# Two stages of a hybrid layer in other forms: neighbourhood attention in larger query tiles, and the spectral products with other PSUM buffers

## The chip, the cores and the metric

The kernel runs on one core of a Trainium2 chip. The metric is the device time of one execution in microseconds (us); for the kernel before it is the median of three runs. Engines are named as in the profile: PE multiplies matrices (PEld is its weight load), DVE and ACT work on vectors, POOL is the general engine, SP issues most DMAs.

## The reference, cut to what matters

The input is four images of 56 x 56 tokens with 128 channels. Each image goes through three residual steps:

```python
# group norm over the image (32 groups), then 7x7 neighbourhood attention, 4 heads of 32:
q, k, v = split(norm(x) @ qkv_w.T + qkv_b)
attn = softmax(einsum("bnhwd,bnhwkd->bnhwk", q, k_win) * SCALE + bias)
x += einsum("bnhwk,bnhwkd->bnhwd", attn, v_win) @ proj_w.T + proj_b
# layer norm, then linear attention with exp features:
q, k, v = exp(h @ Wq + bq), exp(h @ Wk + bk), h @ Wv + bv
x += einsum("bnu,buv->bnv", q, einsum("bnu,bnv->buv", k, v))
# layer norm, then a mixture of experts (hard choice of one of 4) of a spectral filter:
#   16 long causal filters along the 3136 tokens, each with two 128x128 matrices (plus, minus),
#   and an autoregressive part of 3 taps with 128x128 matrices
out = spectral(h, sigma, phi, M_plus, M_minus) + ar(M_u, h)
```

The long convolution is done as a transform over 42 x 56 points: rows first (42 frequencies), then for each of the 42 frequencies a stage with tokens, filters and matrices, then back.

## The kernel before, in words

All data are float32. There are four stages. The *preparation* chooses the expert, forms the filter matrices `mats` in SBUF and the transformed filters `vd` in DRAM. Then each *image* is worked on in turn (`project`, `row_transforms` of the image before, `attend`, `mix`). Then comes the *spectral stage*, 42 iterations. The *last stage* transforms back, adds the stored `td` and writes the output.

*Image.* `load_image` brings an image as `acc` (two buffers, the next image while this one is mixed). `project` turns tokens to channels (`to_channels`, L527), takes group statistics, normalizes, and makes keys `kp` (L658), queries `qT` (L670) and values (L684, L688); the values are stored in DRAM as `vpad`, with a border of zeros. `attend` walks over 35 tiles of 8 rows by 12 or 8 columns. For tile n, `weigh` loads the values of the window from `vpad` in two halves of seven rows (`v_sb`), multiplies the scores of four heads (`sp`, L723, four row groups of the array side by side), adds the bias and takes the maximum in one DVE instruction per head (L736), exponentiates with a sum on ACT (L747) and scales on POOL (L758). `turn_over` transposes the scores of one key half (L770) and copies them (L774, DVE or ACT), `collect` multiplies with the values (L785) and copies the output (L792). PE's order is written out: in step n PE turns over the first half of tile n-2, weighs tile n, turns over the second half of n-2 and collects n-3. Score buffers `st` are four. `mix` adds the projection to `acc` (L543, L552), normalizes (`normed`: statistics on DVE, ten small POOL instructions per block of 512 tokens, normalizing on ACT at L594, all pipelined by block), mixes (L824 to L846), and does the same again for the autoregressive part (L560), storing `ud` and `td` block by block. `row_transforms(b)` reads `ud` back as `uin`, multiplies with `into` (L505), copies `xs` and stores it in `xd`; for image b it stands after the projection of image b+1. Outside the two parts with PE's order written out, a planner orders each engine's instructions: the earliest in the program that it thinks ready.

*Spectral stage.* Iteration `it` has eight steps `eh`. In each, `matrices` makes a sixteenth of the filter matrices' 64 rows by 16 matmuls (L934, four row groups) in two tiles `pg`, each two PSUM banks, one buffer per tile; DVE copies one tile and ACT the other into `gt` (L943). Then come seven `product`s of the iteration before (L953): sixteen rows of `py` in quadrant m2 % 4, two accumulating matmuls each. After sixteen products `gather` copies the four quadrants of the `py` bank (two buffers) to `ys`, by ACT and DVE in turn (L966). `token_points` runs in steps 1 and 3 (L916, copies L924 and L925), `columns` for iteration `it - 3` in step 5 (two matmuls, L989, each with a copy on ACT, L996, through one bank). `regroup` takes `ys` through DRAM (`yd`) to `yg`.

Of the kernel before, what the change touches and what calls it, by code (L numbers as in the profile page):

```python
# [21 lines left out]
QR, QC = 8, 12  # L22
WIDTHS = (12, 12, 12, 12, 8)
# [3 lines left out]
KH = KR // 2  # L27
KMAX = KH * KC
# [92 lines left out]
def hybrid_kernel(  # L121
# [33 lines left out]
    vpad = tc.dram_tile([B, HP, WP, C], F32, name="vpad")  # L155
# [10 lines left out]
    main = ctx.enter_context(ExitStack())  # L166

# [206 lines left out]
    with main as ph:  # L374
        wts = ph.enter_context(tc.tile_pool(name="wts", bufs=1, reuse_waits="tile"))
        res = ph.enter_context(tc.tile_pool(name="res", bufs=2, reuse_waits="tile"))
        img = ph.enter_context(tc.tile_pool(name="img", bufs=1, reuse_waits="tile"))
        work = ph.enter_context(tc.tile_pool(name="work", bufs=2, reuse_waits="tile"))
        small = ph.enter_context(tc.tile_pool(name="small", bufs=4, reuse_waits="tile"))
        ps_s = ph.enter_context(tc.tile_pool(name="ps_s", bufs=3, space=bass.MemoryType.PSUM, reuse_waits="tile"))  # L380
        ps_t = ph.enter_context(tc.tile_pool(name="ps_t", bufs=1, space=bass.MemoryType.PSUM, reuse_waits="tile"))
        ps_m = ph.enter_context(tc.tile_pool(name="ps_m", bufs=1, space=bass.MemoryType.PSUM, reuse_waits="tile"))

        turn = [0]

        def bank():

            turn[0] = (turn[0] + 1) % 4
            if turn[0] == 3:
                return ps_m.tile([P, 512], F32, tag="m", name="bm")  # L390
            return ps_s.tile([P, 2, 512], F32, tag="s", name="bs")[:, 0, :]

        def load_image(b):

            acc = res.tile([P, NB, 2 * C], F32, name="acc")
            nc.sync.dma_start(
                acc[:, : NB - 1, :],
                xt[b, : 256 * (NB - 1)].rearrange("(j p f) c -> p j (f c)", p=P, f=2),
            )
            nc.sync.dma_start(  # L400
                acc[:TAIL, NB - 1, :],
                xt[b, 256 * (NB - 1) :].rearrange("(p f) c -> p (f c)", f=2),
            )
            return acc

        accs = {0: load_image(0)}


        wqkv = wts.tile([P, 3 * C], F32, name="wqkv")
        nc.scalar.dma_start(wqkv, qkv_wT)  # L410
        bqkv = wts.tile([P, 2], F32, name="bqkv")
        with nc.allow_non_contiguous_dma(reason="256 biases, a partition each"):
            nc.scalar.dma_start(bqkv, qkv_b[: 2 * C].rearrange("(s p) -> p s", p=P))
        nc.vector.tensor_scalar(bqkv[:, 0:1], bqkv[:, 0:1], HD ** -0.5, None, ALU.mult)
        bval = wts.tile([P, C], F32, name="bval")
        nc.scalar.dma_start(bval, qkv_b[2 * C :].partition_broadcast(P))
# [5 lines left out]

        relb = {}
        for qc in sorted(set(WIDTHS)):
            kc = qc + KS - 1
            relb[qc] = wts.tile([QR * qc, NH, KR * kc], F32, name=f"relb{qc}")
            for h in range(NH):
                for qy in range(QR):
                    at = (h * BIAS_H + QR - 1 - qy) * BIAS_W + QC - qc
                    nc.scalar.dma_start(  # L430
                        relb[qc][qy * qc : (qy + 1) * qc, h, :],
                        bass.AP(
                            rel_bias.tensor,
                            rel_bias.offset + at,
                            [[1, qc], [BIAS_W, KR], [1, kc]],
                        ),
                    )
# [7 lines left out]
        bkv = wts.tile([P, 2 * C], F32, name="bkv")  # L445
        nc.scalar.dma_start(bkv[:, :C], bk.partition_broadcast(P))
        nc.scalar.dma_start(bkv[:, C:], bv.partition_broadcast(P))
        into = wts.tile([P, 2 * N1], F32, name="into")
        nc.scalar.dma_start(into, table["into"])


# [676 lines left out]
```

## Time and profile before

| | |
|---|---|
| median of three runs | 2739.52 us (2738.39 to 2740.39) |
| the profiled execution's own time | 2739.52 us |
| its span, first to last instruction | 2737.7 us |
| granted TensorE clock, mean | 0.771 |
| busy: PE, PE weight loads, DVE, ACT, POOL | 2069.0, 1419.4, 1331.0, 1072.3, 694.2 us |
| preparation; images; spectral stage; last stage | about 148; 1345; 1094; 151 us |

The stages are cut by eye from the chain of work that ended last. A view of groups gives, for each line of the program, engine and tile, the busy time, the mean of one instruction and the idle time just before it with what ended it; the view of waits sums that idle time by pair; the timeline lists instructions by start; the view of windows gives busy time by engine in a stretch. Matmul durations overlap, so a matmul's cost on the path is read from the distance between starts.

### The profile page before, as it was taken

The numbers are of one execution on the slowest core, as the hardware profiler recorded it, in microseconds if no ns is written. First come the engines' busy times: TensorE is split into PE (matmuls) and PEld (weight loads), VectorE is DVE, ScalarE is ACT, GpSimd is POOL, SyncE is SP. The second block draws the span as 40 slices with busy tenths as digits, with TensorE's granted clock in tenths as the row PEclk, the third lists the DMA queues.
The fourth block names the chain that finished last, engine by engine and source line by source line (L and its number), as shares of the span: only waits on it lengthen the run. The fifth ranks groups of instructions, "written<-read, shape, count | busy, mean of one in ns | idle before, by whom it ended". The sixth has DMA issues, their size and how long they took to land.

```text
span 2737.7 us, 67019 instructions
## 1 busy us (share of the span) xinstructions
PE 2069.0 (76%) x28284; PEld 1419.4 (52%) x28284; DVE 1331.0 (49%) x3228; ACT 1072.3 (39%) x2521; POOL 694.2 (25%) x1227
## 2 busy tenths in 40 slices
PE   3066687666776677776686888888888888888598
PEld 3034456244563445534463767666766666676322
DVE  5244445444454443444432556555555655555232
ACT  0034433344424444244441455555555555555200
POOL 1146734376424664257630000000000000000000
PEclk7565579555885557855585899999999999999755
DMA  6620003300043000420015233333333333333497
GB/s 163 144 88 26 27 1 106 100 26 23 9 113 88 27 19 14 111 66 26 16 44 139 42 81 81 81 81 79 89 78 86 81 86 76 76 80 65 105 229 199
DMA packets 219519, 210.11 MB, mean 77 GB/s; under 512 B 43154, under 2 KB 187250, under 8 KB 218642
## 3 DMA queue, kind: packets, MB, share of 16 engines
q1 hardware_dynamic: 197850, 189.31, 27.9%
q10 hardware_dynamic: 21368, 16.51, 2.3%
q8 instruction: 222, 3.64, 0.5%
q14 instruction: 79, 0.65, 0.1%
HBM read 116.32 MB, written 89.45 MB: 75 GB/s over the span
## 4 chain that ended last, share of the span: by engine, by line
PE 42%; ACT 19%; DVE 18%; DMA 9%; issue 6%; POOL 5%; SPq 1%; ACTq 1%; DVEq 0%; POOLq 0%
ACT st L747 8%; PE pg L934 7%; DVE ys L966 7%; PE py L953 6%; PE sp L723 6%; ACT ys L966 5%; DVE gt L943 5%; PE pt L770 4%; PE bs L543 4%; ACT gt L943 3%; PE po L1059 2%; DMA xd<-xs 2%; DVE st L736 2%; PE pz L989 2%; PE pu L916 2%
## 5 line engine op out<-in xcount | busy, mean ns | idle before, releaser
L758 POOL TENSOR_SCALAR st<-st,rec 96x252 f32<-96x252 f32 (+1 forms) x560 | 484.9, 880 | 370.9 <-DVE rec L756 216.5
L943 DVE COPY gt<-pg 128x896 f32<-128x896 f32 x336 | 366.7, 1091 | 288.4 <-PE pg L934 279.1
L934 PE MATMUL pg<-v,mats 32*128 32x112 f32 x10752 | 398.9, 286 | 103.2 <-DVE gt L943 86.1
L934 PEld LDWEIGHTS pg<-v,mats 32*128 32x128 f32 x10752 | 338.5, 190 | 192.4 <-DVE gt L943 167.1
L747 ACT ACTIVATE st<-st,nmx 96x252 f32<-96x252 f32 (+1 forms) x560 | 270.4, 484 | 351.2 <-DVE nmx L736 351.2
L943 ACT COPY gt<-pg 128x896 f32<-128x896 f32 x336 | 304.4, 906 | 244.7 <-PE pg L934 233.5
L770 PE MATMUL pt<-ident,st 96*126 96x96 f32 (+1 forms) x1120 | 233.8, 360 | 214.6 <-ACT p L774 162.6
L953 PE MATMUL py<-gt,us 128*16 128x128 f32 x9408 | 389.7, 283 | 2.5 <-DVE gt L943 1.6
L770 PEld LDWEIGHTS pt<-ident,st 96*126 96x126 f32 (+1 forms) x1120 | 159.4, 207 | 347.0 <-POOL st L758 252.1
L953 PEld LDWEIGHTS py<-gt,us 128*16 128x16 f32 x9408 | 295.0, 112 | 67.4 <-issue 31.1
L966 DVE COPY ys<-py 16x512 f32<-16x512 f32 (+1 forms) x336 | 209.5, 624 | 160.2 <-ACT ys L966 157.8
L736 DVE CUSTOM_DVE_ANT_0 st<-sp,relb 96x252 f32<-96x252 f32 (+1 forms) x560 | 195.3, 400 | 87.8 <-PE sp L723 87.1
L966 ACT COPY ys<-py 16x512 f32<-16x512 f32 (+1 forms) x336 | 174.6, 520 | 149.2 <-DVE ys L966 141.1
L723 PE MATMUL sp<-kp,qT 32*96 32x252 f32 (+1 forms) x1120 | 162.2, 647 | 3.3 <-DVE xs L185 1.8
L774 DVE COPY p<-pt 126x384 f32<-126x384 f32 (+1 forms) x140 | 74.2, 530 | 160.3 <-PE pt L770 160.3
L594 ACT ACTIVATE hn<-acc,v 128x128 f32<-128x128 f32 (+1 forms) x208 | 88.1, 484 | 153.2 <-POOL v L586 138.9
L1059 PE MATMUL po<-z,onto 84*56 84x512 f32 x224 | 126.0, 1066 | 21.8 <-DMA z<-zd 21.8
L989 PE MATMUL pz<-yg,back 112*112 112x512 f32 x168 | 96.5, 657 | 46.3 <-ACT zs L996 36.2
L785 PE MATMUL po<-p,v_sb 126*32 126x96 f32 (+1 forms) x2240 | 112.6, 349 | 0.8 <-DVE aT L792 0.8
L505 PE MATMUL px<-uin,into 28*84 28x512 f32 x224 | 77.0, 960 | 36.2 <-DVE xs L185 19.7
L747 ACT ACTIVATION_READ_ACCUMULATOR st<-st,nmx 96x1 f32 (+1 forms) x560 | 104.4, 186 | 0.0
L1068 DVE SCALAR_TENSOR_TENSOR tl<-po,hmask,tl 56x512 f32<-56x512 f32 x56 | 42.0, 750 | 124.3 <-PE po L1059 123.7
(162 smaller groups left out, 2221.3 us busy)
## 6 DMA issues: line engine op xcount, KB each, us to landing
xd<-xs SPq DMA_DIRECT2D x112, 168.0 KB
xm<-xd SPq DMA_DIRECT2D x84, 224.0 KB
yd<-ys SPq DMA_DIRECT2D x168, 112.0 KB
yg<-yd SPq DMA_DIRECT2D x84, 224.0 KB
zd<-zs SPq DMA_DIRECT2D x84, 224.0 KB
z<-zd SPq DMA_DIRECT2D x14, 1344.0 KB
v_sb<-vpad SPq DMA_DIRECT2D x224, 63.0 KB
vpad<-vt SPq DMA_DIRECT2D x56, 112.0 KB
```

Of the source, the lines that this page charges most:

```text
L723: nc.tensor.matmul(sp[h // 2][:nq, h % 2, : 2 * kn], qT[hs, ty, QR * x0 : QR * x0 + nq], kp[hs, y0 : y0 + KR, x0 : x0 + kc], start=True, s ...
L736: nc.vector.tensor_tensor_reduce(st[:nq, h, : 2 * kn], sp[h // 2][:nq, h % 2, : 2 * kn], relb[qc][:, h], -1.0, 3.0e38, ALU.add, ALU.min, n ...
L747: nc.scalar.activation(st[:nq, h, : 2 * kn], st[:nq, h, : 2 * kn], AF.Exp, bias=nmx[:nq, h : h + 1], scale=-1.0, accum_out=ssum[:nq, h : h ...
L758: nc.gpsimd.tensor_scalar(st[:nq, h, : 2 * kn], st[:nq, h, : 2 * kn], rec[:nq, h : h + 1], None, ALU.mult)
L770: nc.tensor.transpose(pt[:kn, h, :nq], st[:nq, h, c * kn : (c + 1) * kn], ident[:nq, :nq])
L785: nc.tensor.matmul(po[hs], v_sb[:kn, c, hs], pc[c][:kn, h, :nq], start=(c == 0), stop=(c == 1),)
L934: nc.tensor.matmul(pg[g // 2][:, g % 2, 2 * N2 * i : 2 * N2 * (i + 1)], mats[rows, 4 * eh + i, :], v[rows], start=True, stop=True,)
L943: copy(gt[:, :, e0 : e0 + 8, :].rearrange("p m (g i) c -> p g m i c", g=2), pg[q][:, :, : 8 * N2].rearrange("p g (i m c) -> p g m i c", i= ...
L953: nc.tensor.matmul(py[32 * j : 32 * j + 2 * NSB, slot, :], us[:, 1 - c : 3 - c, :, m2], gt[:, m2, :, c], start=(c == 0), stop=(c == 1),)
L966: (nc.vector.tensor_copy if j % 2 else nc.scalar.copy)(ys[rows, 4 * q : 4 * q + n], py[rows, :n])
L989: nc.tensor.matmul(pz, tables_of(m1)[2], yg[:, s * B : (s + 1) * B].rearrange("p k e -> p (k e)"), start=True, stop=True,)
L1059: nc.tensor.matmul(po[64 * q : 64 * q + H].rearrange("p b c -> p (b c)"), onto[:, s], zin[q][:, i, s], start=(s == 0), stop=(s == NS - 1),)
```

## The change

Both the image stage and the spectral stage take other forms.

*Images.* All four images are loaded at the very start into one `acc`. Attention has 28 tiles of 8 x 14 queries; the keys of a tile are 14 x 20 and are turned over in three chunks of 5, 5 and 4 rows. Values stay in SBUF as `vp` in channels; for each tile POOL copies the window, PE transposes it in three parts, and DVE copies the result. Scores are taken two heads at a time; one DVE instruction scales and adds the bias for both, one takes the maximum, ACT exponentiates, DVE scales. PE's order in attention is left to the planner. A layer norm takes all statistics of the image first (DVE), then one power (POOL), then normalizes all blocks (DVE). `row_transforms(b)` stands at the end of image b, and `td` is stored in two DMAs just before it.

*Spectral.* `pg` has three rotating buffers of two banks, of which a step uses two; each is copied by DVE (one bank) and ACT (the other). `py` has one buffer; products come eight at a time in steps 0 to 6, with 32 columns of `us` (16 wanted, 16 of other rows or zeros) so that all 128 rows of the bank are written, and one full-width copy, alternating between ACT and DVE, takes the bank. `columns` does one half in step 5 and one in step 7, with alternating copies, and shares its bank with `token_points`.

```diff
-QR, QC = 8, 12
-WIDTHS = (12, 12, 12, 12, 8)
+QR, QC = 8, 14
...
+    acc = keep1.tile([P, NB, B, 2 * C], F32, name="acc")
+    for b in range(B):
+        nc.sync.dma_start(acc[:, : NB - 1, b, :], xt[b, : 256 * (NB - 1)]...)
...
+        ps_s = ...bufs=2  ps_t = ...bufs=2  ps_m = ...bufs=2      (ps_s tiles are two banks)
...
+        def layer_norm(b, to):
+            for j in range(NB):
+                r = rows_of(j)
+                for f in range(2):
+                    g = 2 * j + f
+                    nc.vector.bn_stats(stats[:r, g, :], acc[:r, j, b, f * C : (f + 1) * C])
+                    nc.vector.bn_aggr(mv[:r, g, :], stats[:r, g, :])
+            nc.gpsimd.tensor_scalar(rstd, mv[:, :, 1], LN_EPS, None, ALU.add)
+            nc.gpsimd.tensor_tensor(rstd, rstd, mhalf, ALU.pow)
+            for js in BLOCKS:
+                hn = work.tile([P, 2, 2, C], F32, name="hn")
...
+                        nc.vector.tensor_scalar(hn[...], acc[...], mv[:r, g, 0:1],
+                            rstd[:r, g : g + 1], ALU.subtract, ALU.mult)
+                to(js, lambda j, f: hn[:r, j - js[0], f, :], hn)
...
+            def weigh(ty, tx):
+                vt = work.tile([P, KR, KC], F32, name="vt")
+                nc.gpsimd.tensor_copy(vt, vp[:, y0 : y0 + KR, x0 : x0 + KC])
+                pv = ps_m.tile([KMAX, len(RCH), C], F32, tag="m", name="pv")
+                for c, nr in enumerate(RCH):
+                    nc.tensor.transpose(pv[: nr * KC, c, :], vt[...], ident)
+                nc.vector.tensor_copy(v_sb[:, 0:2, :], pv[:, 0:2, :])
+                nc.vector.tensor_copy(v_sb[:nk2, 2, :], pv[:nk2, 2, :])
+                for hp in range(NH // 2):
+                    sp = ps_s.tile([NQ, 2, 512], F32, tag="s", name="sp")
+                    for hh in range(2):
+                        nc.tensor.matmul(sp[:, hh, :NK], qT[hs, ty, tx]..., kp[hs, ...], ...)
+                    st = work.tile([NQ, 2, NK], F32, name="st")          # two buffers
+                    nc.vector.scalar_tensor_tensor(st, sp[:, :, :NK], HD ** -0.5, relb[...], ALU.mult, ALU.add)
+                    nc.vector.tensor_reduce(nmx, st, AX.X, ALU.max, negate=True)
+                    for hh in range(2):
+                        nc.scalar.activation(st[:, hh, :], st[:, hh, :], AF.Exp, bias=..., accum_out=...)
+                    nc.vector.reciprocal(rec, ssum)
+                    for hh in range(2):
+                        nc.vector.tensor_scalar(st[:, hh, :], st[:, hh, :], rec[:, hh : hh + 1], None, ALU.mult)
+                    pt0 = ps_t.tile([KMAX, 2, 2, NQ], F32, tag="t", name="pt0")
+                    pt1 = ps_t.tile([nk2, 2, NQ], F32, tag="t", name="pt1")
...                                                       (six transposes into pt0 and pt1)
+                    nc.scalar.copy(p0, pt0)
+                    nc.vector.tensor_copy(p1, pt1)
...
+            for ty in range(H // QR):
+                for tx in range(W // QC):
+                    now = weigh(ty, tx)
+                    if before is not None:
+                        collect(*before)
+                    before = now
...
+            layer_norm(b, autoregress)
+            nc.sync.dma_start(td[b, ...], acc[:, : NB - 1, b, :])
+            nc.sync.dma_start(td[b, ...], acc[:TAIL, NB - 1, b, :])
+            row_transforms(b)
...
-        ps_g = ...bufs=1     ps_y = ...bufs=2
+        ps_g = ...bufs=3     ps_y = ...bufs=1
...
-            for q, copy in enumerate((nc.vector.tensor_copy, nc.scalar.copy)):
-                e0 = 16 * eh + 8 * q
-                copy(gt[:, :, e0 : e0 + 8, :]..., pg[q][:, :, : 8 * N2]...)
+            for q in range(2):
+                for g, copy in enumerate((nc.vector.tensor_copy, nc.scalar.copy)):
+                    e0 = 16 * eh + 8 * q + 4 * g
+                    copy(gt[:, :, e0 : e0 + 4, :], pg[q][:, g, : 8 * N2]...)
...
-                    py[32 * j : 32 * j + 2 * NSB, slot, :],
-                    us[:, 1 - c : 3 - c, :, m2],
+                    py[32 * j : 32 * (j + 1), slot, :],
+                    us.rearrange("p c k m -> p (c k) m")[:, NSB * (1 - c) : NSB * (5 - c), m2],
...
+                    if eh in (5, 7) and 0 <= az < N1:
+                        columns(az, ygs[az], zs, eh // 6)
+                    if 0 <= ap < N1 and eh < 7:
+                        if eh % 2 == 0:
+                            py = ps_y.tile([P, 4, C], F32, name="py")
+                        for m2 in range(8 * eh, 8 * eh + 8):
+                            product(py, gts[ap], us2[ap % 2], m2)
+                        if eh % 2 or eh == 6:
+                            q, n = eh // 2, 2 if eh == 6 else 4
+                            evacuate(ys[:, 4 * q : 4 * q + n], py[:, :n])
```

## The prediction

> **What bounds the kernel now.** I read the busy times by window first, with the windows cut where the chain of waits changes its lines. The columns are: window, its length, busy us of PE, PE's weight loads, DVE, ACT and POOL, then the granted clock, DMA share and GB/s.
>
> ```profile
> 182.00:348.00 166.00, 112.13 (x1031) 66.77 (x1034) 80.38 (x401) 79.19 (x303) 118.22 (x136) 0.51 0.09 25
> 348.00:452.00 104.00, 85.05 (x524) 66.80 (x521) 42.78 (x125) 37.78 (x91) 41.02 (x146) 0.83 0.12 37
> 452.00:511.00 59.00, 41.96 (x166) 19.98 (x164) 26.80 (x46) 13.29 (x23) 8.80 (x13) 0.73 0.54 147
> 1530.00:2550.00 1020.00, 898.01 (x20319) 704.55 (x20314) 603.48 (x731) 522.07 (x810) 0.00 (x0) 1.00 0.35 78
> ```
>
> These are attention of image 0, its two norms with the mixing between, projection of image 1 with the row transforms of image 0, and the spectral stage. Images 1 to 3 repeat the first three (attention 170, 166, 167; projection 59, 59, 57). So 148 us of preparation, about 1345 for the images, 1094 for the spectral stage (1493 to 2587), 151 for the end. In attention POOL is the busiest (118 of 166: `L758`, 0.9 us each, four a tile) and no engine is full: 35 tiles take 4.8 us each at half clock. In the spectral stage PE is busy 88% at full clock, so I looked at the waits there (who waited for whom: us in total, times, longest):
>
> ```profile
> DVE ys L966 <- ACT ys L966: 157.8, 289, 4.2
> ACT ys L966 <- DVE ys L966: 141.1, 166, 1.2
> PEld pg L934 <- DVE gt L943: 167.1, 252, 3.5
> PEld pz L989 <- ACT zs L996: 72.7, 42, 2.3
> ACT xs L183 <- DMA xd<-xs: 86.8, 23, 6.6
> ```
>
> The timeline of one iteration shows how they hang together (start, us, what):
>
> ```profile
> 1910.75 0.57 ACT L966 COPY ys<-py 16x512 f32<-16x512 f32 x1
> 1911.03 0.98 PEld L934 LDWEIGHTS pg<-v,mats 32*128 32x128 f32 x32 [0.37 <-DVE gt L943]
> 1911.03 1.16 PE L934 MATMUL pg<-v,mats 32*128 32x112 f32 x32
> 1911.35 0.68 DVE L966 COPY ys<-py 16x512 f32<-16x512 f32 x1 [0.37 <-ACT ys L966]
> 1912.07 0.58 ACT L966 COPY ys<-py 16x512 f32<-16x512 f32 x1 [0.75 <-DVE ys L966]
> ...
> 1912.67 0.70 DVE L966 COPY ys<-py 16x512 f32<-16x512 f32 x1 [0.64 <-ACT ys L966]
> 1913.40 1.09 DVE L943 COPY gt<-pg 128x896 f32<-128x896 f32 x1
> ```
>
> The four quarter copies of one product bank go one after another, ACT, DVE, ACT, DVE, 2.6 us from 1910.75 to 1913.37. DVE's copy of the filter matrices, whose matmuls ended at 1912.1, starts only at 1913.40, and with one pair of banks per half the next matrices wait for it. The first token-point matmul comes at 1900.67 and again at 1925.85: 25.2 us an iteration.
>
> [...] the quarter copies are in different quadrants and still take turns. [...] 128x448 from PSUM takes 0.62 us (`L924`), 128x1024 in SBUF 0.75 (`L296`)[...].
>
> **The change, part by part.**
>
> *Spectral stage.* One iteration's PE work after the change: eight sets of filter matrices at 1.09 us (1902.84 to 1903.93, no stall), eight; seven groups of products instead of eight. A group of seven products takes 1.09 (1901.75 to 1902.84) and its longest quadrant has two products; a group of eight has two in each quadrant, so it also costs 1.09. Then two token-point blocks at 1.07 and two column matmuls at about 0.95. Sum 8.7 + 7.6 + 2.1 + 1.9 = 20.4. The stationary operand of a product grows from 16 to 32 columns. [...] I take 0.4, since in attention 32-column loads of `po` show matmuls exactly one stream apart (0.160 us). With 0.8 us of small gaps: 21.6 us against 25.2, 3.6 x 42 = **-151**. The copies do not stand in the way: DVE has sixteen 128x448 at 0.62, two 128x512 at 0.69, two `us` at 0.62 and one `zs` at 0.6, 13.2 us; ACT sixteen at 0.55 and the rest, about 11. A pair of banks is free 0.75 us after its matrices (0.1 + 0.62), and 1.09 of products or 0.95 of columns cover that; if both engines lag, the third pair covers one more. The single `py` bank must be emptied within the 1.09 of the next matrices (0.7 needed). Ends: -175 if no gap is left, -110 if loads and waits keep 1 us more.
>
> *Attention.* 28 tiles of 112 queries by 280 keys in place of 35 of at most 96 by 252. At half clock, from the trace's spacing: a transpose costs 0.160 for 96 columns, so 0.187 for 112 and 0.213 for 128; a score pass 0.528 for 252 keys with its 96-column load, so 0.588 for 280 and 112; each switch between kinds about 0.14. PE per tile: three transposes of values 0.78 with the switch; scores in two head pairs, each two passes of two heads, 2 x (2 x 0.588 + 0.05) = 2.45, where four heads went side by side before in 1.1; twelve transposes in four groups, 12 x 0.187 + 4 x 0.14 = 2.80; output, four heads side by side, six passes each, 6 x 0.187 + 0.14 = 1.26. **Sum 7.3.** DVE: per pair one scale-and-add over 560 (0.75 for 512 at `L1068`, so 0.80), one reduction over 560 (0.607 for 448 at `L624` and 1.04 ns an element more: 0.72), a reciprocal 0.16, two multiplies (0.75 less 744 elements at 0.52 ns: 0.36 each), one copy of 224 (0.39): 2.79, twice, with values 0.72 and output 0.26: 6.6, or 5.5 where neighbours overlap by 0.07. ACT 3.2; POOL one copy, about 0.7. Two score buffers of a pair each (four of two pairs before) give 5.6 us a tile at least: 0.80 + 0.72 + exp 1.2 + 0.16 + 0.72 + transposes 1.4 and six hand-overs of 0.1. The order on PE is no longer written out. PE at 7.3 with 0.4 of waits makes 7.7 us a tile: 28 x 7.7 = 216 against 167, +48.4 x 4 = **+193**. Ends: 6.4 (score pairs side by side, DVE sets the pace), +48; 8.6, +294. The clock I leave at 0.5[...].
>
> *Norms.* POOL's small instructions and ACT's normalizing go; DVE gets 26 aggregates (about 0.2, from 0.345 for 42 elements) and 26 multiplies (about 0.3) per norm, and nothing is normalized before all statistics are in and one power over 26 columns is done (0.57 for 1 column, 1.04 for 4: about 4.5 us). First norm about 16 + 5 + 11, second 16 + 5 + 25 against 35 and 40 us now; the mixing between is bound by PE as before. That is 3 us more[...], +10 an image, **+40** (0 to +80).
>
> *Row transforms.* They move from behind the next image's projection to ahead of it. Their 28 stores of 168 KB fill 28 us at 173 GB/s, and PE, ACT and DVE have nothing else meanwhile (`xs` waiting for `xd`). After the change the projection uses other banks and may run beside them. But the `td` stores, seven per image now, become two of 1.6 MB in all on SP's queue after the last block, and the four `uin` loads stand behind them: about 12 us before the transforms start; and PE's queue holds projection behind transforms that wait for stores. 12 + 28 = 40 us instead of 58, three times: **-54** (0 to -90). The last transforms stay exposed (43).
>
> *Start.* Four images (6.3 MB) go ahead of the preparation's loads on SP's queue; one took 9.9 us, so 30 to 40 us later for everything behind. Against that, SP's late load of image 0 (9.9), 32 of 64 bias loads (0.47 us each on ACT's queue) and 16 stores of zeros (7) go from the end of the same chain: **0** (-20 to +20). The 224 + 56 loads of values from DRAM and 56 stores vanish; they were hidden (DMA share 0.09, and PE waited 0.4 us for `v_sb` in all), worth nothing. In the spectral stage the `zd` stores move behind the `yg` loads on SP; nobody waits for them before the last stage.
>
> Sum: -151 + 193 + 40 - 54 + 0 = +28. The profiled execution took 2739.52 us around a span of 2737.7, and is itself the median; so 2739.5 + 28 = **2768**.
>
> **Rivals.** *Score pairs side by side* (0.26): PE issues both pairs' scores together, a tile takes 6.2 to 7.2. At 6.7: 28 x 6.7 = 188, +81; sum -84, **2655, faster**. The sign turns where 112 tiles at t less 669 equal 151 + 54 - 40: t = 7.45 us. For it: four of eight PSUM banks are for scores, and nothing orders the pairs apart. Against: a pair's bank comes free only behind its own scale-and-add, 1.5 us after the other's. *Queues in step* (0.15): with two score buffers PE, DVE and ACT wait for each other in turn; 8.6 us, **2868**. Now the busiest engine reaches only 71% with four buffers. *The spectral gain is eaten* (0.07): `py` alone in its bank, or the wider loads, take the place of the removed waits; -60 instead of -151, **2859**.
>
> **How the numbers follow.** Forecast 0.52 (a tile 7.2 to 8.2, 2710 to 2825; of this 0.10 faster, 0.05 same, 0.37 slower). With the rivals: faster 0.35, same 0.05, slower 0.60. The ends of the parts (95, 25, 35, 40, 20) taken as independent give 113 about the sum: 2655 to 2880, which leaves about 1 in 10 on each side. A change of 0.2% (5.5 us) is about what a measurement of this kernel can tell from none.
>
> **What would show it.** Right: spectral iterations of about 21.6 us with no `ys` waiting for `ys`; attention windows near 216 us at clock 0.5 with PE busy over 85%; project and transforms 40 us. Wrong: a tile under 7.45 us, a clock near 1.0 in attention (PE then halves and DVE's 6.6 sets the pace), or `pg` still waiting for `gt`.

## The result, and the profile after

The changed kernel takes **2979.44 us** (median of four runs, 2974.23 to 2980.09), the kernel before 2738.95 in the same session: ratio 1.0874, 95% interval 1.0855 to 1.0893. The forecast was 2768, with a range to 2880: slower was right, the size was not. The profiled execution took 2980.09 us around a span of 2978.3, against 2739.52 and 2737.7.

Both spans, cut at the same four events (first score product, last copy of an attention output, first token-point product, end), in us:

| stretch | before | after | measured | predicted |
|---|---|---|---|---|
| start to the first scores | 179.8 | 168.1 | -12 | 0 |
| attention, first score to last output, four images | 716 | 1095 | **+379** | +193 |
| norms, mixing, projection, row transforms | 602 | 612 | +10 | +40 - 54 = -14 |
| first token-point product to the end | 1240 | 1103 | -136 | -151 |
| sum | 2737.7 | 2978.3 | +241 | +28 |

So 186 of the 213 us of error lie in attention. Windows of the changed kernel, cut by the same events (window, length, busy us of PE, PE's loads, DVE, ACT, POOL, granted clock, DMA share, GB/s): attention of image 0, its norms and mixing, projection of image 1 with the row transforms of image 0, and the spectral stage.

```profile
168.00:441.00 273.00, 252.18 (x1320) 146.19 (x1319) 156.16 (x420) 93.73 (x281) 10.94 (x26) 0.51 0.00 1
441.00:547.00 106.00, 75.79 (x425) 61.54 (x426) 58.21 (x229) 16.64 (x42) 9.92 (x7) 0.81 0.09 27
547.00:599.00 52.00, 44.06 (x141) 16.99 (x139) 25.75 (x43) 16.81 (x25) 10.25 (x16) 0.80 0.48 132
1910.00:2796.00 886.00, 883.87 (x20235) 728.81 (x20225) 506.15 (x848) 426.90 (x848) 0.00 (x0) 1.00 0.40 90
```

PE is now the full engine in both large stages: 92% of attention, at half clock, and 99.8% of the spectral stage, at full clock. The chain of work that ended last, by line, says where:

```profile
PE po L706 15%; PE pg L842 13%; PE py L862 12%; PE pt L685 8%; PE pa L511 5%; PE pu L824 3%; PE pz L887 3%; PE pt L690 3%; PE pv L634 3%; DVE nmx L665 2%; PE pq L610 2%; DMA z<-zd 2%; DMA out_dram<-tl 2%; PE pk L739 2%; DVE p L696 1%
```

The output products of attention (`po`), 1.26 us a tile in the prediction, hold 15% of the chain: some 440 us, 4 us a tile. The timeline of PE over one tile of the changed kernel (start, length of the group, what, and the idle time before it):

```profile
298.32 0.58 PE L685 MATMUL pt<-ident,st 112*100 112x112 f32 x2 [0.18 <-DVE st L678]
...
300.09 0.61 PE L685 MATMUL pt<-ident,st 112*100 112x112 f32 x2 [0.44 <-DVE p L696]
300.49 0.39 PE L690 MATMUL pt<-ident,st 112*80 112x112 f32 x1
300.81 0.58 PE L706 MATMUL po<-p,v_sb 100*32 100x112 f32 x2
301.33 0.61 PE L685 MATMUL pt<-ident,st 112*100 112x112 f32 x2
301.73 0.39 PE L690 MATMUL pt<-ident,st 112*80 112x112 f32 x1
302.06 1.34 PE L706 MATMUL po<-p,v_sb 100*32 100x112 f32 x10
303.33 0.46 PE L634 MATMUL pv<-ident,vt 128*100 128x128 f32 x1
303.71 0.95 PE L706 MATMUL po<-p,v_sb 100*32 100x112 f32 x4
304.60 0.45 PE L634 MATMUL pv<-ident,vt 128*100 128x128 f32 x1
304.98 1.33 PE L706 MATMUL po<-p,v_sb 80*32 80x112 f32 x8
306.24 0.43 PE L634 MATMUL pv<-ident,vt 128*80 128x128 f32 x1
306.61 1.29 PE L648 MATMUL sp<-kp,qT 32*112 32x280 f32 x8
308.08 0.58 PE L685 MATMUL pt<-ident,st 112*100 112x112 f32 x2 [0.18 <-DVE st L678]
```

A tile repeats after 9.76 us (298.32 to 308.08), and the distances between starts give its parts (a group's length runs into the next one's: 302.06 + 1.34 is 303.40, the next starts at 303.33): the 24 output passes 0.52 + 1.27 + 0.89 + 1.26 = 3.94, cut into four pieces by the transposes; twelve transposes 2.78; value transposes 1.13, one at a time; all eight score passes together 1.29; waits 0.44 + 0.18.

In the spectral stage the waits of the prediction are gone. Of the changed kernel's list of waits (who waits for whom: us, times, longest) the lines that answer to those of before:

```profile
ACT gt L852 <- DVE gt L852: 467.9, 336, 7.0
DVE gt L852 <- PE pg L842: 320.7, 335, 3.1
ACT xs L194 <- DMA xd<-xs: 49.3, 16, 9.8
DVE xs L196 <- DMA xd<-xs: 45.3, 16, 4.2
PEld pg L842 <- ACT gt L852: 17.8, 49, 2.2
```

No `ys` waits for `ys`, and PE's loads wait 18 us for `gt` instead of 167. The first line is new: ACT's copy of one bank of a pair waits for DVE's copy of the other bank. An iteration takes 21.9 us (25.2 before).

### The profile page after: what moved, and what is told of

Its sections match the earlier page's. It is cut to its first block, busy times and chain, and to the rows that moved or that the text cites. A ratio compares the mean times of both kernels' runs of the same rounds, so it can differ in the third digit from the quotient of the medians.

```text
span 2978.3 us, 66692 instructions
## 1 busy us (share of the span) xinstructions
PE 2562.0 (86%) x28900; PEld 1717.5 (58%) x28900; DVE 1576.6 (53%) x3797; ACT 955.9 (32%) x2271; POOL 151.3 (5%) x245
## 4 chain that ended last, share of the span: by engine, by line
PE 73%; DVE 13%; DMA 8%; issue 2%; POOL 1%; ACT 1%; SPq 1%; ACTq 0%; DVEq 0%
PE po L706 15%; PE pg L842 13%; PE py L862 12%; PE pt L685 8%; PE pa L511 5%; PE pu L824 3%; PE pz L887 3%; PE pt L690 3%; PE pv L634 3%; DVE nmx L665 2%; PE pq L610 2%; DMA z<-zd 2%; DMA out_dram<-tl 2%; PE pk L739 2%; DVE p L696 1%
## 5 line engine op out<-in xcount | busy, mean ns | idle before, releaser
L852 DVE COPY gt<-pg 128x448 f32<-128x448 f32 x672 | 388.1, 619 | 323.9 <-PE pg L842 320.7
L852 ACT COPY gt<-pg 128x448 f32<-128x448 f32 x672 | 357.6, 533 | 467.9 <-DVE gt L852 467.9
L706 PE MATMUL po<-p,v_sb 100*32 100x112 f32 (+1 forms) x2688 | 464.8, 393 | 1.7 <-ACT p L695 1.7
L862 PE MATMUL py<-gt,us 128*32 128x128 f32 x9408 | 370.8, 293 | 3.0 <-DVE ys L196 1.7
L668 ACT ACTIVATE st<-st,nmx 112x280 f32<-112x280 f32 x448 | 232.8, 520 | 403.5 <-DVE rec L676 309.6
L706 PEld LDWEIGHTS po<-p,v_sb 100*32 100x32 f32 (+1 forms) x2688 | 280.8, 159 | 130.1 <-issue 117.0
L862 PEld LDWEIGHTS py<-gt,us 128*32 128x32 f32 x9408 | 297.2, 145 | 62.2 <-issue 31.1
L685 PE MATMUL pt<-ident,st 112*100 112x112 f32 x896 | 262.8, 399 | 77.3 <-DVE p L696 45.8
L690 PE MATMUL pt<-ident,st 112*80 112x112 f32 x448 | 175.5, 392 | 0.0
L656 DVE SCALAR_TENSOR_TENSOR st<-sp,relb 112x560 f32<-112x560 f32 x224 | 163.2, 728 | 0.2
```

Source lines behind the costliest of these rows:

```text
L656: nc.vector.scalar_tensor_tensor(st, sp[:, :, :NK], HD ** -0.5, relb[:, 2 * hp : 2 * hp + 2, :], ALU.mult, ALU.add,)
L668: nc.scalar.activation(st[:, hh, :], st[:, hh, :], AF.Exp, bias=nmx[:, hh : hh + 1], accum_out=ssum[:, hh : hh + 1],)
L685: nc.tensor.transpose(pt0[:, hh, c, :], st[:, hh, c * KMAX : (c + 1) * KMAX], ident[:NQ, :NQ],)
L690: nc.tensor.transpose(pt1[:, hh, :], st[:, hh, 2 * KMAX :], ident[:NQ, :NQ])
L706: nc.tensor.matmul(po[hs].rearrange("c y x -> c (y x)"), v_sb[: nr * KC, c, hs], p0[:, h % 2, c, :] if c < 2 else p1[:, h % 2, :], start=( ...
L852: copy(gt[:, :, e0 : e0 + 4, :], pg[q][:, g, : 8 * N2].rearrange("p (i m c) -> p m i c", i=4, c=2),)
```

## Experiments

"Written order" below means that PE's order in attention stands in the program, as it did before the change. Times are medians; ratios are to the kernel before, timed in the same session.

### Attention: the order of PE's work

**Output products in turn.** In the changed kernel:

```diff
-for h in range(NH):
-    for c, nr in enumerate(RCH):
+for c, nr in enumerate(RCH):
+    for h in range(NH):
         nc.tensor.matmul(po[hs], v_sb[: nr * KC, c, hs], ...)
```

> The changed kernel (2979 us), with the two loops around its output products exchanged: the key chunk is the outer loop and the head the inner one, so that neighbouring products go to different 32-column quarters of the array, as in the kernel before. Theory (the 24 output passes of a tile run one after another because six in a row share a quarter; they cost about 4 us where four heads side by side would cost 1.3): a tile falls from 9.1 to 6.4 to 7.2 us, the attention window from 254 to 180 to 202 us, the whole by 210 to 300 us, to 2680 to 2770. Rival (score buffers and the hand-overs between PE, DVE and ACT set the pace at about 8.6 us, and the full PE only hides it): a tile stays at 8.6 or more, the whole at 2910 or more. Rival (32-column weight loads set the pace of these passes whatever their order): under 30 us.

Measured: 2922.04 us, ratio 1.0668 (1.0647 to 1.0690), 57 us less instead of 210 to 300; attention 262 us. (The 9.1 and 254 us of the expectation come from a window cut too short; by the events they are 9.76 and 273.) One tile of PE in this run:

```profile
304.26 0.58 PE L685 MATMUL pt<-ident,st 112*100 112x112 f32 x2 [0.56 <-DVE st L678]
...
308.51 0.88 PE L634 MATMUL pv<-ident,vt 128*100 128x128 f32 x3
309.32 1.27 PE L648 MATMUL sp<-kp,qT 32*112 32x280 f32 x2
310.52 1.33 PE L706 MATMUL po<-p,v_sb 100*32 100x112 f32 x20
311.78 1.28 PE L648 MATMUL sp<-kp,qT 32*112 32x280 f32 x6
313.63 0.40 PE L685 MATMUL pt<-ident,st 112*100 112x112 f32 x1 [0.56 <-DVE st L678]
```

The output did get cheaper: 20 passes in 1.26 us, all 24 in 2.28. But the planner, given other loops, made another order: the score passes, eight in 1.29 us before, are now two and six and take 1.20 + 1.29, followed by a wait of 0.56. A tile takes 9.37 us. The theory was right on the passes and wrong on what they are worth, because one edit changed two orders.

**The order written out**, with the chunk outside (first run) and with the head outside (second):

```diff
+with tc.manual_schedule(engines={mybir.EngineType.PE}):
+    for n in range(len(tiles) + 2):
+        scores(n); turn_over(n - 1, pair 0); values(n); turn_over(n - 1, pair 1); collect(n - 2)
-for ty ...: for tx ...: now = weigh(ty, tx); collect(*before)
```

> The changed kernel (2979 us; a tile of attention repeats every 9.76 us, attention of an image 273 us) with the same instructions, but PE's order in attention written out: in step n all eight score passes of tile n, transposes of pair 0 of tile n-1, the value transposes of tile n, transposes of pair 1 of tile n-1, then the output of tile n-2 with chunk outside and head inside. Theory (PE's order costs the time: 24 output passes on one column quarter after another, and in the run with the loops exchanged the score pairs pulled apart by the planner): per tile 1.5 scores + 2.8 transposes + 0.8 values + 1.4 output = 6.5, with waits 6.5 to 7.4 us, attention 185 to 210 us, the whole 2690 to 2760. Rival (two score buffers and the hand-overs set the pace once PE is freed): 8.2 us a tile or more, the whole 2830 or more.

> The same written order, but the output product with the head outside and the chunk inside, six passes in a row on each column quarter. This parts the output's order from the planner's. Theory (the serial passes cost 2.6 us of PE, and PE is the bound): 9.0 to 9.8 us a tile, 230 to 300 us more than with the chunk outside, the whole 2950 to 3020. Rival (the planner's other choices, not the output's order, cost the time): within 60 us of the run with the chunk outside.

Measured: **2568.70 us**, ratio 0.9372 (0.9356 to 0.9389), and **2546.03 us**, ratio 0.9294 (0.9280 to 0.9308). The same instructions in another order take 411 and 433 us off; attention falls from 273 to 168 and 166 us. This is far below the theory's 2690, and serial passes, which were to cost 230 us, cost nothing. The edit does two things: it writes PE's order, and it moves the program's own order (a pair is turned over one tile later, the output comes two tiles later), from which the planner orders the other engines. The new program order with PE left to the planner was not run, so the two are not told apart. PE in the run with the chunk outside:

```profile
185.24 1.35 PE L725 MATMUL po<-p,v_sb 100*32 100x112 f32 x24
186.52 1.29 PE L638 MATMUL sp<-kp,qT 32*112 32x280 f32 x8
...
191.02 0.39 PE L705 MATMUL pt<-ident,st 112*80 112x112 f32 x1
191.34 0.79 PE L725 MATMUL po<-p,v_sb 100*32 100x112 f32 x24
```

and the output passes of two neighbouring tiles in the run with the head outside:

```profile
252.26 1.43 PE L725 MATMUL po<-p,v_sb 100*32 100x112 f32 x24
257.81 2.47 PE L725 MATMUL po<-p,v_sb 100*32 100x112 f32 x24
```

Two things are to be seen. First, in one piece the 24 passes take 1.28 us (chunk outside) or 2.40 (head outside) at half clock, where the planner's pieces took 3.94; a tile at half clock falls from 9.76 to 6.10 us (185.24 to 191.34). Second, the same instructions take 0.72 or 1.36 us a little later: **the clock changes between half and full** within attention, while in the changed kernel it stays at half there. At full clock a tile takes 5.5 us in both runs, with DVE busy 33.2 of 34 us (220 to 254, head outside), so there the serial passes cost nothing; at half clock a tile with the head outside takes about 6.9 us (257.81 to 264.73), so with it the full clock is part of the gain. The windows from 200 to 310 us, first with the chunk outside, then with the head outside, show the clock as the last number but two:

```profile
200.00:310.00 110.00, 93.60 (x891) 58.06 (x891) 102.47 (x283) 60.51 (x187) 7.99 (x19) 0.71 0.01 1
```

```profile
200.00:310.00 110.00, 87.33 (x922) 59.15 (x921) 104.75 (x291) 62.37 (x194) 8.13 (x20) 0.94 0.01 1
```

**What grants the clock.** The records give the clock in steps of 3.413 us. I took each step as a window and added up in it the array work of all matrix passes, rows x columns x streamed length as the profile prints them, as a share of what 128 x 128 passes fill a window with at half clock: one of 128 columns takes 213 ns there (the median distance between the starts of 211 passes of `L543` in the kernel before), so 33.6 million. Over 3022 windows, from 150 to 1440 us of the two kernels, the three runs above, the spectral stage alone and the two runs on row transforms, "full clock if the window before had at least 0.62" holds in 95%; without the transposes the best threshold holds in 90%, with PE's busy share in 66%, and always guessing half in 64%. In attention, from 200 to 310 us:

```
run                        us a tile   array work per window: mean, largest   clock
before                         4.8       0.39   0.58                          0.50
changed                        9.76      0.36   0.49                          0.50
output in turn                 9.37      0.38   0.43                          0.50
written, chunk outside      5.5 - 6.1    0.60   0.79                          0.71
written, head outside       5.5 - 6.9    0.62   0.73                          0.94
```

A tile holds 34.7 million (34.9 in the expectation below): in 9.76 us that never reaches 0.62 however busy PE looks (0.49 at most), in 6.1 us it sometimes does (0.79 at most). The fit is rough: the last two rows differ by 0.02 in work and by 0.23 in clock, and in the five later runs with a written order the same 0.62 holds in 90% of 1890 windows, with the value copies on ACT in only 75%. What else decides stays open. The fit is a correlation, so work was added to test it: per tile four transposes of the identity, or two products (two passes each, as the 12 output products of a tile are 24 passes in the records; the same array work), into columns of the output's bank that nobody reads:

```diff
 po = pw[:, :NQ]
+for _ in range(4): nc.tensor.transpose(pw[:, 128:256], ident, ident)
+# or, in the second run
+for _ in range(2): nc.tensor.matmul(pw[:, 128:256], ident, ident, start=True, stop=True)
```

> The run with PE's order written out and the chunk outside (2569 us, mean clock 0.71 to 0.75 in attention, 5.5 us a tile where the clock is full and 6.1 to 6.9 where it is half), with four more 128 x 128 x 128 transposes of the identity per tile ahead of the output passes, into columns of the output's bank that nobody reads. Theory (the clock granted to a window of 3.4 us follows the array work in the window before, rows times columns times length of all passes, transposes too, with a threshold at about 0.62 of what half clock can carry): per tile 34.9 million cells become 43.3, no window falls under the threshold, the clock is over 0.95 in attention, a tile stays at 5.5 to 5.7 us, the whole 2515 to 2550. Rival (transposes don't count as work): the clock stays at 0.75 or less, and the added 0.4 to 0.8 us of PE makes the whole 2575 to 2640.

> The same with two more 128 x 128 x 128 products (two passes each, so the same array work as four transposes) instead of the four transposes. Theory (all array work counts alike): within 10 us of the run with the four transposes, clock over 0.95, 2515 to 2550. Rival (only products count): this one is faster than the run with transposes by 30 us or more.

Measured: 2539.08 us (ratio 0.9267, 0.9244 to 0.9291) and 2536.82 us (0.9261, 0.9237 to 0.9285): wasted work takes 30 and 32 us off, 22 and 23 of them in the attention of the four images by the traces (673 us to 650), and the two kinds count alike. The run with transposes:

```profile
200.00:310.00 110.00, 84.35 (x1009) 55.22 (x1009) 106.53 (x297) 63.97 (x199) 7.98 (x19) 0.94 0.01 1
```

The clock is 0.94 (0.71 without; a little under the 0.95 expected), and PE, with more to do, is busy for less time. The rival, in which transposes don't count as work and the clock stays at 0.75 or less, did not hold.

**What holds the tile then.** The copies of turned values to ACT, in the written order with the head outside:

```diff
-nc.vector.tensor_copy(v_sb[:, 0:2, :], pv[:, 0:2, :])
+nc.scalar.copy(v_sb[:, 0:2, :], pv[:, 0:2, :])
```

> The run with the written order and six passes in a row per head (2546 us), with the two copies of the turned values moved from DVE to ACT (0.42 and 0.28 us a tile). Theory (where the clock is full DVE is the bound, 9.7 of 10 us busy): a tile falls from 5.5 to about 4.9 us, 28 x 4 x 0.6 = 65 us less at best, 2480 to 2515. Rival (the loop of scores, softmax and transposes through two score buffers is as long): 2530 to 2550.

Measured: 2545.60 us, ratio 0.9290 (0.9260 to 0.9320): nothing gained. The clock is full from 200 to 310 us and DVE busy 97 of the 110, yet a tile takes 5.48 us, 5.52 before, so DVE's load alone is not what holds it. The last run below tries the loop through the score buffers.

### Spectral stage

**The stage alone**, in the kernel before:

```diff
-(spectral stage of the kernel before: pg in two pairs, py in two banks, quarter copies)
+(spectral stage of the changed kernel, whole; images and all else as before)
```

> The kernel before (2739 us) with the whole spectral stage of the changed one and nothing else. Theory (the spectral gain stands by itself): 954 us for the stage instead of 1094, an iteration 22.0 instead of 25.2 us, the whole 140 us less, 2590 to 2610, below both kernels. Rival (part of the measured gain came from what the other image stage left behind, such as where its stores ended): less than 110 us, above 2630.

Measured: **2606.85 us**, ratio 0.9516 (0.9502 to 0.9530), 131 us less; 21.9 us an iteration. The gain stands by itself, a few us under the 140.

**Its parts, one at a time**, in the kernel before. Copies split between the engines:

```diff
-for q, copy in enumerate((nc.vector.tensor_copy, nc.scalar.copy)):
-    copy(gt[8 matrices of pair q], pg[q])
+for q in range(2):
+    for g, copy in enumerate((nc.vector.tensor_copy, nc.scalar.copy)):
+        copy(gt[4 matrices], pg[q][:, g])
```

> The kernel before (2739 us) with one part of the spectral change: each of its two pairs of filter-matrix banks is copied by DVE (one bank) and ACT (the other), instead of DVE one pair and ACT the other. Theory (the removed waits were those of the product bank's four quarter copies, and the split alone frees nothing, since a step's copies take DVE 1.24 us instead of 1.09): -25 to +15 us. Rival (the split frees the first pair early enough to be most of the gain): 80 us or more less.

and 32-column products with the full-width copy:

```diff
-py[32 * j : 32 * j + 2 * NSB, slot, :], us[:, 1 - c : 3 - c, :, m2]
+py[32 * j : 32 * (j + 1), slot, :], us[16 wanted and 16 other rows, m2]
-for j in range(NG): copy(ys[quarter j], py[quarter j])   # ACT and DVE in turn
+evacuate(ys[:, 4 * q : 4 * q + n], py[:, :n])
```

> The kernel before (2739 us) with the other part: products with 32 columns, so that all 128 rows of the bank are written, and one full-width copy by ACT or DVE in turn instead of four quarter copies one after another. The groups stay at seven products a step, two product banks, two filter-matrix pairs, each copied by one engine. Theory (the chain of quarter copies, 2.6 us four times in an iteration, held up the copies of the filter matrices): 60 to 110 us less, the rest of the 132 measured for the whole stage coming from the third pair of banks and the groups of eight. Rival (the filter matrices' banks are the bound): under 30 us less, or slower[...].

Measured: 2867.55 us, ratio 1.0457 (1.0440 to 1.0474), 126 us **slower**, which neither side of the expectation had; and 2668.09 us, ratio 0.9734 (0.9720 to 0.9749), 73 us faster, as the theory said. An iteration takes 28.3 and 23.5 us. The waits of the kernel with split copies:

```profile
ACT gt L944 <- DVE gt L944: 487.8, 295, 8.9
PEld pg L934 <- ACT gt L944: 217.7, 417, 3.5
DVE ys L967 <- ACT ys L967: 166.5, 292, 4.3
PE pg L934 <- ACT gt L944: 118.4, 291, 3.3
```

The two copies of one pair go one after the other, though they are on two banks and two engines. It is the program that orders them: 671 of ACT's 672 copies wait for the semaphore that DVE's copies raise, here as in the changed kernel, where in the kernel before they wait for PE's. With two pairs the next matrices wait for the second copy: 218 us on PE's loads, where the kernel before had 167. So the three pairs without the split were tried:

```diff
 ps_g = tc.tile_pool(name="ps_g", bufs=3, ...)
-for q in range(2): (DVE one bank, ACT the other)
+for q, copy in enumerate((nc.vector.tensor_copy, nc.scalar.copy)):   # one engine a pair
```

> The kernel before with the changed spectral stage (2607 us, 21.8 us an iteration), but each pair of filter-matrix banks copied by one engine, DVE or ACT in turn, as before, with the three rotating pairs kept. Theory (splitting a pair costs, since ACT's copy waits for DVE's of the same pair, as 127 us lost with two pairs showed; the third pair only hides it): 2590 to 2620, no worse than with the split. Rival (the split is needed for the gain): 2640 or more.

Measured: **2588.25 us**, ratio 0.9450 (0.9425 to 0.9474), 21.6 us an iteration: 19 us faster than with the split, 16 of them in the stage by the traces. No `gt` waits for `gt` here; of the loads' wait, most of what is left is

```profile
PEld pg L941 <- ACT gt L950: 44.1, 120, 0.8
```

The gain of the stage is the full-width copy (73 us) and the rest of the new form; the split is a cost that the third pair hides but for 19 us. The rest is more than one thing. From the start of one group of PE's work to the next, waits included, an iteration's products take 11.28 us in the kernel before, 9.84 with the full-width copy and 8.33 here; its two columns take 3.03, 2.83 and 2.08; its matrices 8.72, 8.72 and 9.02. So of the last 1.96 us, 0.75 (some 31 us in all) come from the columns in two steps instead of one behind the other; the third pair and the groups of eight were not taken apart.

### Row transforms

**Behind the next projection** in the program, as before the change:

```diff
             (keys, queries and values of image b)
+            if b > 0: row_transforms(b - 1)
             (attention of image b)
-            row_transforms(b)
```

> The changed kernel (2979 us) with the row transforms of image b put back behind the projection of image b+1, where the kernel before has them. Theory (the move itself was worth nothing, because a transform's stores and its two buffers set the length in either place): the stretch from the end of the second norm to attention stays within 5 us of 59, the whole within 15 us of 2979. Rival of the prediction (ahead of the projection is better by 18 us an image): 40 to 60 us slower. Rival (ahead is worse, because PE's queue holds the projection behind transforms that wait for stores): 20 to 45 us faster.

**A third buffer for their results:**

```diff
-xs = work.tile([2 * N1, 2, 4, C], F32, name="xs")
+xs = work.tile([2 * N1, 2, 4, C], F32, name="xs", bufs=3)
```

> The changed kernel (2979 us) with three buffers for the row transforms' results instead of two; four small buffers of the norms' statistics get one copy instead of two to make room. Theory (each copy waits for the store of two copies before to land, some 3.2 us a copy, so one more store in flight takes off up to a third): the stretch of 59 us falls to 47 to 52, the last transforms from 45 to about 35, the whole by 25 to 45 us. Rival (the DMA queues are full at that rate, or PE's order holds the transforms back): under 10 us.

Measured: 3004.12 us, ratio 1.0939 (1.0873 to 1.1005), and 2974.77 us, ratio 1.0833 (1.0761 to 1.0905). The single runs of both spread by 40 us, so no difference to the changed kernel under some 20 us can be read from the times; the traces say more. PE in the first:

```profile
563.04 18.89 PE L610 MATMUL pq<-xc,wqkv 128*128 128x448 f32 x42 [1.44 <-DVE xc L603]
581.86 1.08 PE L473 MATMUL px<-uin,into 28*84 28x512 f32 x2
...
604.84 3.32 PE L473 MATMUL px<-uin,into 28*84 28x512 f32 x8 [0.97 <-ACT xs L194]
608.92 1.28 PE L650 MATMUL sp<-kp,qT 32*112 32x280 f32 x4 [0.76 <-ACT xs L194]
```

Behind, projection takes 19 us and the transforms 27 after it; from the last attention output to the next scores the three stretches are 162, 158 and 162 us, ahead 158, 151 and 154. So the move brought 6 us an image, 18 in all, a third of the forecast. With three buffers the stores of image 0 take 37 us instead of 45, but the stretches stay at 155, 156 and 155: the stores were not what ended last. Ahead, projection and transforms stand in one queue, and a projection product behind a transform that waits for its store waits too. In the changed kernel:

```profile
570.13 1.02 PE L610 MATMUL pq<-xc,wqkv 128*128 128x448 f32 x2
571.60 1.01 ACT L194 COPY xs<-px 84x1024 f32<-84x1024 f32 x1 [1.76 <-DMA xd<-xs]
572.66 1.09 PE L473 MATMUL px<-uin,into 28*84 28x512 f32 x4 [1.51 <-ACT xs L194]
573.68 1.21 PE L610 MATMUL pq<-xc,wqkv 128*128 128x448 f32 x2
```

### Joined

Written order with two more products, and unsplit copies in three pairs; beside it the same with three score buffers and the value copies on ACT:

```diff
+(written order, two dummy products, one engine a pair of pg)        # both runs
-st = work.tile([NQ, 2, NK], F32, name="st")
+st = work.tile([NQ, 2, NK], F32, name="st", bufs=3)     # second run only
+(the two copies of the turned values by nc.scalar.copy)  # second run only
```

> The run with the written order and two more products per tile (2537 us), with the filter-matrix pairs in the spectral stage copied whole by one engine each (three rotating pairs), which took 19 us off with the images of the kernel before. Theory (the two parts are apart in time and add up): 2510 to 2525 us. Rival (the gain of unsplit copies came with the state in which the images of the kernel before leave things): 2530 or more.

> That run with three buffers for score pairs instead of two, and the copies of the turned values on ACT. Theory (a pair's scores wait for the transposes of the tile before to free its buffer, so scores, maximum, exponent, scaling and transposes form a loop of 5.3 us; a third buffer opens it): a tile falls from 5.4 to 4.7 to 5.0 us, 45 to 75 us less than the run beside it. Rival (PE's written order itself, which turns a pair over only after the scores of the next tile, closes the loop whatever the buffers): within 15 us of it.

Measured: **2520.31 us**, ratio 0.9203 (0.9189 to 0.9217), and 2525.25 us, ratio 0.9223 (0.9208 to 0.9238). The parts add up, and the first is the fastest version found: 218 us below the kernel before. The third buffer brings nothing: the second run's clock is lower (0.88 against 0.94 from 200 to 310 us), but where it is full a tile still takes 5.44 us, against 5.52, so the loop is not opened by it either. What holds a tile there, with DVE busy 96.7 of 110 us in the second run, stays open. Of what PE's matmuls wait for in these 110 us, a DVE copy of turned scores comes first,

```profile
PE pt L705 <- DVE p L711: 21.1, 19, 1.4
```

some 1.1 us a tile; the order of DVE's own instructions was not tried.

## Why the prediction was wrong

**Attention, +193, measured +379: the step that failed.** It is the sum of PE per tile, 7.3 plus 0.4 of waits, against 9.76 measured. By its terms: output 1.26 against 3.94 (+2.68), values 0.78 against 1.13 (+0.35), scores 2.45 against 1.29 (-1.16), transposes 2.80 against 2.78, waits 0.4 against 0.62. "Output, four heads side by side" took over the order of the kernel before; in the changed loop the head is outside, so neighbouring passes share a quarter of the array, and the planner cut them into four pieces between transposes. The score pairs did go side by side, as a rival said, and by luck hid over 1 us of the error.

Behind the term stands the sentence "the order on PE is no longer written out", to which I gave only 0.4 us of waits. The runs show that the order is the whole loss: with it written out the changed tiles need 165 to 169 us an image, less than the 177 to 181 of the kernel before. With the chunk outside, 28 tiles of 6.1 us at half clock are 171 us, as 35 of 4.8 are 168, and 6.1 is about my sum of 7.3 with the score pairs side by side. (With the head outside they would be 193, and the full clock makes up for it.) So the edits that I priced one by one (larger tiles, transposed values, two score buffers) cost next to nothing together. DVE's terms were near: scale-and-add over 560 takes 0.728 us (0.80 in the sum), the reduction 0.724 (0.72), a multiply over 280 0.358 (0.36). For their 1.04 and 0.52 ns an element the traces show 1.05 (448 and 896 copied from PSUM in the kernel before, 0.619 and 1.091 us) and 0.53 (multiplies over 280 here and 1024 before, 0.358 and 0.750 us).

**The clock.** "The clock I leave at 0.5" was right for this kernel: 0.51, as before the change. That it stayed at half fits the work, 34.7 million cells in 9.76 us. More transposes are no reason for a low clock here: four added ones a tile raised it from 0.71 to 0.94, two products to 0.95. The case named as "a clock near 1.0 in attention (PE then halves and DVE's 6.6 sets the pace)" nearly came when the order was written out: clock 0.94, the output passes at 1.36 us where they take 2.40 at half clock, 5.5 us a tile, DVE almost always busy. But taking 0.7 us of copies off DVE did not shorten the tile.

**Spectral stage, -151, measured -136.** Mechanism right in the main: no `ys` waits for `ys`, PE full, 21.9 us an iteration against 21.6. But I took the split of the copies as part of the gain ("free 0.75 us after its matrices"); it costs 19 us, since the two copies of a pair take turns. By its parts an iteration is 9.37 us of matrices, 8.34 of products, 2.15 of token points and 2.08 of columns; the sum had 8.7, 7.6, 2.1 and 1.9, with 0.4 for loads and 0.8 for gaps, so that the total came this near is in part luck. (The 0.4 was an estimate with no measured cost of a wider load behind it, and near: a group of seven products takes 1.16 us with the wider loads, in the full-width run, and 1.09 before, 0.5 us an iteration.) One reading was off: in the stretch that I showed, the next matrices do not wait for DVE's copy, which ends at 1914.49. They start at 1916.25, behind two columns through one bank:

```profile
1914.11 1.11 PE L989 MATMUL pz<-yg,back 112*112 112x512 f32 x2 [0.88 <-ACT zs L996]
```

**Row transforms, -54, measured -18.** The overlap came. I had named what limits it ("PE's queue holds projection behind transforms that wait for stores") but gave it no time, and priced the 28 stores at 28 us (168 KB each at 173 GB/s, the rate of the kernel before from 1450 to 1493 us), where image 0's are issued over 45. **Norms**, +40: the stretches with both together give +10, so with -18 for the move about +28, in the range; of my 10 us an image 3 were sums of instructions and 7 a guess at what a lower clock would cost (it went from 0.83 to 0.81 in the windows of image 0); the power over 26 columns took 4.51 us, as forecast. **Start**, 0: -12.

**Sign and range.** Slower held, for the expected reason (PE per tile over 7.45 us), but at 9.76 us a tile, above even the 8.6 of the slower rival. The range took 95 us for attention, where its own ends, +48 and +294, lie 145 and 101 from +193; with these it would be wider, and still not reach 2979.

## What to carry to other kernels

When an edit hands an engine's order from the program to a planner, price the order, not only the instructions: here the same instructions in two orders differ by 433 us of 2979. Before assuming a clock, add up the array work in 3.4 us, transposes included, which the clock followed in 95% of the windows of the fit here; a PE that looks 92% busy at half clock may be thinly filled (0.36 of what half clock carries here), and packing its passes into one piece can win twice, in the passes (3.94 to 2.40 us a tile at half clock, head outside in both) and in the clock (0.50 to 0.94 from 200 to 310 us). Two engines that share one tile's copies may be made to take turns by the program; look at which semaphore the second waits for, and try a whole tile for each.

## What the hardware showed that I had not expected

- The clock mostly followed the array work of the window of 3.413 us before: 0.62 of what half clock carries, as the limit for full clock, is right in 95% of 3022 windows of the fit and in 90% of 1890 later ones. Four added 128 x 128 x 128 transposes a tile raised it from 0.71 to 0.94, as two products of the same work did (0.95), and the kernel became 30 us faster.
- 24 output passes with 32-column weights and 112 streamed columns at half clock: 1.28 us when neighbours are in different quarters (written order, chunk outside), 2.40 when six in a row share one (head outside), 3.94 when these are also cut into four pieces by transposes (changed kernel).
- A turn-taking that looks like the hardware's was the program's: copies by DVE and ACT from two banks of one tile ran one after the other, since the second waits for the first one's semaphore (671 of 672 times in the changed kernel); with two pairs of banks that cost 126 us, with three 19.
